# Turning an attention block's rows by transposing transfers of 16-bit planes, with scores two tiles ahead

## The chip, the cores and the metric

The kernel runs on one core of a Trainium2 chip. The metric is the device time of one launch in microseconds (us), lower is better. The core has a matrix engine (TensorE, here PE, with its weight loads as PEld), three elementwise engines (VectorE or DVE, ScalarE or ACT, GpSimd or POOL), and sixteen DMA engines that are fed through the queues of the issuing engines, here mostly SyncE (SP) and ScalarE. Each engine runs its instructions in order; they wait for each other through semaphores.

## The reference

The input x has 4 batches of 1024 rows of 1024 numbers. A recurrent stage makes new rows from x and a side input, by two scans along the 1024 positions (one forward, one backward), a division and a gate. Those rows then pass twice through the same attention over 16 slots per batch, and the result is added to x:

```python
for _ in range(NB):                      # NB = 2 blocks
    logits = _rms(x, norm_pre_w) @ compete_w.T + compete_b
    vals, idx = jax.lax.top_k(jnp.swapaxes(logits, 1, 2), 4)
    wgt = jax.nn.softmax(vals, axis=-1)
    wx = x @ write_w.T + write_b
    written = einsum('bsk,bskd->bsd', wgt, take_along_axis(wx, idx))
    ws = _rms(ws + written, norm_post_w)
    q  = x @ wq.T + bq                   # 16 heads of 64
    kk = ws @ wk.T + bk
    vv = ws @ wv.T + bv
    att = softmax(einsum('blhd,bshd->bhls', q, kk) * scale)
    ctx = einsum('bhls,bshd->blhd', att, vv)
    x = _rms(x + ctx @ out_proj_w.T + out_proj_b, norm_post_w)
```

All numbers are 32-bit floats. `_rms` divides a row by the root of its mean square and multiplies by a weight.

## The kernel before, in words

There are three stages: the recurrence (function bodies up to line 720), and then, for each of the two blocks, `write_slots` (the choice of rows, the slots, and the maps that attention needs) and `attention`. Before attention `write_slots` folds the query projection into the keys (`km`, 1024 by 256 for a batch, and 16 more columns in the first block for the next logits) and the output projection into the values (`vm`, 256 by 1024). So a tile of 128 rows needs two products only: its scores, rows times `km`, and its outputs, weights times `vm`. There are 32 tiles a block.

The order on every engine is the order in which the code is written (`pin`). The work on one tile g is:

- `load` (L1070): SP loads the rows `y`, and in the first block also the turned rows `xt`, 512 KB each. The turned rows are needed because PE contracts over the partitions. The recurrence makes them anyway and stores them in `turned_rows`. Three tiles are loaded in `begin_loads`; in the loop tile g + 3 is loaded in the pass of tile g.
- `turn_rows` (L1078), in the second block only: PE transposes the eight 128x128 squares of `y` (tile `ptr`), and ACT copies them from PSUM to `xt` in two copies.
- `scores` (L1090): PE, eight accumulated products into the bank `psc`.
- `softmax` and `softmax_sum` (L1104, L1121): DVE adds the bias, takes the maximum of each head and subtracts it; ACT takes the exponential; DVE sums and inverts; POOL multiplies.
- `turn_weights` (L1134): PE transposes the two squares of weights (`pet`), ACT copies them beside the weights.
- `output` (L1144): PE, two halves of two accumulated products into two banks `po`; DVE adds each half to `y`. The first block also computes the next logits (`poc`).
- `norm` (L1191): ACT sums the squares, DVE and POOL make the inverse root, DVE scales `y`. In the first block SP stores `y` to `rows[1]`, where the second block loads it from; in the second block POOL adds x (`xin`) and SP stores to the output.

In the pass of tile g, `run` (L1262) issues the loads for g + 3, the scores and softmax of g + 1, the outputs of g, the turned weights of g + 1 and the norm of g. In the second block the rows of g + 2 are turned between the scores of g + 1 and the outputs of g. Before the loop, `begin` does the scores and softmax of tile 0, and `early` turns the rows of tiles 0 and 1 of the second block while the rows chosen for the slots are being gathered.

SP runs its transfers in order as well: within one pass these are the loads, a weight load for the next block in some passes (`load_ahead`), and the store of the tile's rows after its norm. The row buffers are five, the buffers for turned rows three, those for scores and weights (`half`) two, those for 1 MB pieces of weights (`wide`) nine. `hold_clock` issues matmuls whose result nobody uses.

Of the kernel before, what the change touches and what calls it, by code (L numbers as in the profile page):

```python
# [11 lines left out]
U32 = mybir.dt.uint32  # L12
AF = mybir.ActivationFunctionType
# [5 lines left out]
P = 128  # L19
# [5 lines left out]
NT = L // P  # L25
# [13 lines left out]
def kernel(  # L39
# [37 lines left out]

    pin = tc.keep_in_program_order
# [7 lines left out]
    def wide(name):  # L86
        return weights.tile([P, 2, D], F32, tag="wide", bufs=9, name=name)
# [171 lines left out]
    with rec_stack:  # L259
# [276 lines left out]
        for i in range(N):  # L536
# [22 lines left out]
            if N // 2 - 2 <= i < N // 2 + 8 and i % 2 == 0:  # L559
                load_ahead(0, (i - N // 2 + 2) // 2)  # L560
            if i == N - 1:
                for n in range(5, 9):
                    load_ahead(0, n)
# [164 lines left out]
    def half_row(name):  # L728
        return work.tile([P, 2 * C + S], F32, tag="half", bufs=2, name=name)[:, : D // 2]
# [7 lines left out]
    def write_slots(blk, begin_loads, early, begin):  # L737
# [72 lines left out]
        hold_clock(bank("po", f"idle_rows{blk}"), 5 if first else 1)  # L810
# [33 lines left out]
        for n in range(5, NJ):  # L844
            wkv.append(load_kv(n, blk))
# [214 lines left out]
    def attention(blk):  # L1060
# [7 lines left out]
        lg_ps, maps = {}, {}  # L1068
# [9 lines left out]
        def turn_rows(g):  # L1078

            ptr = [turned(f"ptr{g}_{h}") for h in range(2)]  # L1080
            for h in range(2):
                for q in range(4):
                    pin(nc.tensor.transpose(ptr[h][:, q, :], y[g][:, ts(4 * h + q, P)], ident))  # L1083
            xt_g[g] = trow(f"xt{blk}_{g}").rearrange("p (k c) -> p k c", c=P)
            return [
                lambda h=h: pin(nc.scalar.copy(xt_g[g][:, 4 * h : 4 * h + 4, :], ptr[h]))
                for h in range(2)
            ]
# [15 lines left out]
        def softmax(g):  # L1104

            n = f"{blk}_{g}"
            two[g] = work.tile([P, 2 * C + S], F32, tag="half", bufs=2, name=f"e{n}")
            e = two[g][:, :C]
            w = C if last else C + S
            pin(nc.vector.tensor_add(two[g][:, :w], psc[g][:, :w], score_bias[:, g // NT, :w]))  # L1110
            e3 = e.rearrange("p (h s) -> p h s", s=S)
            mx = small.tile([P, H], F32, tag="mx", name=f"mx{n}")
            pin(nc.vector.tensor_reduce(mx, e3, AX.X, ALU.max))
            pin(
                nc.vector.tensor_tensor(
                    e3, e3, mx.unsqueeze(2).to_broadcast([P, H, S]), ALU.subtract
                )
            )
            pin(nc.scalar.activation(e, e, AF.Exp))
# [14 lines left out]
        def turn_weights(g):  # L1134
            if last:
                pet = bank(("aux", "lg")[g % 2], f"pet{blk}_{g}", 1)[:, :C]
            else:
                pet = turned(f"pet{blk}_{g}").rearrange("p q c -> p (q c)")[:, :C]
            pet = pet.rearrange("p (q c) -> p q c", c=P)
            for h in range(2):  # L1140
                pin(nc.tensor.transpose(pet[:, h, :], two[g][:, ts(h, P)], ident))  # L1141
            pin(nc.scalar.copy(two[g][:, C + S :].rearrange("p (h t) -> p h t", h=2), pet))  # L1142
# [106 lines left out]
        def early():  # L1249

            if last:
                for g in range(2):
                    for copy in turn_rows(g):
                        copy()

        def begin(km):
            maps["km"] = km
            scores(0)
            softmax(0)
            softmax_sum(0)  # L1260

        def run(vm, vmc):  # L1262
            maps["vm"], maps["vmc"] = vm, vmc
            turn_weights(0)
            for g in range(N + 1):
                here, next_, past = g < N, g + 1 < N, g > 0
                if g + 3 < N:
                    load(g + 3)
                if here and last:
                    xin[g] = fat(f"xin{g}")  # L1270
                    move(xin[g], x[g // NT, ts(g % NT, P), :])
                if not last and 4 <= g < 4 + 2 * 9 and g % 2 == 0:
                    load_ahead(blk + 1, (g - 4) // 2)
                if past and here and not last:
                    total_n = square_sum(y[g - 1], f"n{g - 1}")
                if next_:
                    scores(g + 1)
                    turn = last and g + 2 < N
                    if turn:
                        copies = turn_rows(g + 2)  # L1280
                        copies[0]()
                    softmax(g + 1)
                    if turn:
                        copies[1]()
                if past and next_ and not last:
                    inv_n = inverse_root(total_n, f"n{g - 1}")
                if next_:
                    softmax_sum(g + 1)
                if past and here and last:
                    pin(nc.gpsimd.tensor_add(y[g - 1], y[g - 1], xin[g - 1]))  # L1290
                    move(out[(g - 1) // NT, ts((g - 1) % NT, P), :], y[g - 1])
                if next_ and past and not last:
                    next_logits(g - 1, inv_n)
                if here:
                    output(g)
                if past and not last:
                    if here and not next_:
                        next_logits(g - 1, inverse_root(total_n, f"n{g - 1}"))
                    turn_logits(g - 1)
                    if here and not next_:  # L1300
                        hold_clock(bank("po", "idle_norm"), 4)
                if next_:
                    turn_weights(g + 1)
                if here:
                    (norm if next_ else norm_last)(g)
# [60 lines left out]
```

## Time and profile before

The time is 1098.41 us, the median of three runs (1097.13 to 1103.73).

| | |
|---|---|
| profiled execution's own time | 1097.41 us |
| its span, first to last instruction | 1095.6 us |
| instructions | 11962 |
| granted clock of PE, mean | 0.962 |
| DMA traffic | 218.79 MB, 200 GB/s over the span |
| first block's attention | about 508 to 756 us |
| second block's attention | about 816 to 1092 us |

A line of the profile's groups names the source line, the engine and the operation, the tiles (written <- read) with their shape, the number of such instructions, and the time of one. In an answer in order of time the first number is the start in us from the start of the span and the second the length; the square bracket gives the idle time of the engine before and what ended it. "SPq" is SP issuing a transfer: its length is the time to issue, and the landing is told apart. The chain of waits is the path that ended last, followed back from the end.

### The profile page before, as it was taken

Reading aid. Unit: us, or ns where it says so; the run is one execution under the profiler, and the core shown is the slowest. Engines: PE = TensorE matmul, PEld = TensorE weight load, DVE = VectorE, ACT = ScalarE, POOL = GpSimd, SP = SyncE. Lnnn points to the kernel's source line nnn. Section 1 sums busy time; section 2 is a strip of 40 time slices with the busy share of each in tenths; the row PEclk is TensorE's granted clock in tenths of the full one; section 3 lists DMA queues with packets and bytes.
Section 4 is the critical chain, followed back from the end, with each engine's and each line's share of the span. In section 5 each row is a group of like instructions: output and inputs, shape, how many; then the busy total and the mean of one; then the engine's idle time right before and its main releaser. Section 6 shows DMA issues by size and latency. Waiting matters only on the chain.

```text
span 1095.6 us, 11962 instructions
## 1 busy us (share of the span) xinstructions
PE 972.7 (89%) x4156; PEld 541.9 (49%) x4156; DVE 767.0 (70%) x1049; ACT 507.5 (46%) x787; POOL 546.4 (50%) x417
## 2 busy tenths in 40 slices
PE   2688788877878788899999999998999999999996
PEld 0123222222323233584666666664584676766763
DVE  7999999999999995144666666656144555555555
ACT  5476777768676763012334444444123333333332
POOL 4999999999999882100222222222100444434444
PEclk9789899989989899999999999999999999999999
DMA  8575574856564265790577777553760454545554
GB/s 272 181 261 170 155 225 128 281 153 232 171 212 129 82 200 156 256 355 16 203 277 281 267 253 273 205 200 120 282 260 20 149 216 179 213 188 208 192 210 154
DMA packets 121788, 218.79 MB, mean 200 GB/s; under 512 B 10928, under 2 KB 76592, under 8 KB 121728
## 3 DMA queue, kind: packets, MB, share of 16 engines
q1 hardware_dynamic: 87872, 199.15, 51.3%
q10 hardware_dynamic: 33280, 16.78, 5.3%
q0 software_dynamic: 576, 2.10, 0.5%
q8 instruction: 33, 0.54, 0.2%
q14 instruction: 27, 0.22, 0.1%
HBM read 150.90 MB, written 67.11 MB: 199 GB/s over the span
## 4 chain that ended last, share of the span: by engine, by line
PE 58%; DVE 31%; issue 4%; POOL 3%; ACT 2%; DMA 1%; SPq 0%; POOLq 0%; DVEq 0%; ACTq 0%
DVE both L320 22%; PE psc L1095 20%; PE po L1152 19%; DVE both L419 3%; DVE ov L364 3%; PE ptr L1083 3%; PE pk L955 3%; PE pkv L885 3%; PE pv L1023 2%; PE pet L1141 1%; PE pw L835 1%; PE raw L442 1%; PE poc L1168 1%; PE num L370 1%; PE pmix L817 1%
## 5 line engine op out<-in xcount | busy, mean ns | idle before, releaser
L1095 PE MATMUL psc<-km,xt 128*128 128x272 f32 (+1 forms) x1024 | 238.4, 386 | 0.0
L1152 PE MATMUL po<-vm,e 128*128 128x512 f32 x512 | 230.4, 593 | 0.9 <-ACT e L1142 0.9
L1095 PEld LDWEIGHTS psc<-km,xt 128*128 128x128 f32 x1024 | 189.5, 190 | 29.1
L370 PE MATMUL num<-ov,minus_ident 128*128 128x512 f32 x128 | 88.6, 831 | 97.6 <-DVE ov L364 97.6
L1129 POOL TENSOR_TENSOR e<-e,den 128x256 f32<-128x256 f32 x64 | 40.5, 633 | 252.5 <-DVE den L1127 231.4
L320 DVE TENSOR_TENSOR_SCAN both<-columns,edges,both 128x1024 f32<-128x1024 f32 x64 | 148.2, 2316 | 0.0
L1152 PEld LDWEIGHTS po<-vm,e 128*128 128x128 f32 x512 | 94.8, 190 | 95.7 <-issue 85.4
L1193 DVE SCALAR_TENSOR_TENSOR y<-y,inv,npost_bc 128x1024 f32<-128x1024 f32 x62 | 79.6, 1285 | 41.2 <-POOL inv L1188 41.2
L1161 DVE TENSOR_TENSOR y<-po,y 128x512 f32<-128x512 f32 x128 | 85.8, 674 | 30.9 <-PE po L1152 30.6
L1181 ACT ACTIVATE junk<-y 128x1024 f32<-128x1024 f32 x63 | 66.7, 1058 | 69.2 <-DVE y L1193 69.1
L370 PEld LDWEIGHTS num<-ov,minus_ident 128*128 128x128 f32 x128 | 28.2, 244 | 134.3 <-issue 67.7
L1188 POOL TENSOR_TENSOR inv<-mean,minus_half 128x1 f32<-128x1 f32 x64 | 35.5, 555 | 96.8 <-DVE mean L1186 96.8
L412 POOL TENSOR_TENSOR both<-both,quo 128x1024 f32<-128x1024 f32 (+1 forms) x33 | 75.7, 2295 | 14.9 <-ACT quo L399 14.0
L308 POOL TENSOR_TENSOR ekv<-ek,kf 128x1024 f32<-128x1024 f32 (+1 forms) x33 | 75.6, 2293 | 2.6
L1142 ACT COPY e<-pet 128x256 f32<-128x256 f32 x64 | 23.8, 371 | 113.1 <-PE pet L1141 112.9
L413 POOL TENSOR_TENSOR gate<-gate,quo 128x1024 f32<-128x1024 f32 (+1 forms) x33 | 75.3, 2283 | 0.0
L431 POOL TENSOR_TENSOR gate<-gate,both 128x1024 f32<-128x1024 f32 x31 | 73.3, 2366 | 1.2
L1290 POOL TENSOR_TENSOR y<-y,xin 128x1024 f32<-128x1024 f32 x31 | 73.1, 2358 | 1.4 <-DVE y L1193 1.4
L320 DVE TENSOR_TENSOR_SCAN both<-columns,ek 128x1024 f32<-128x1024 f32 (+1 forms) x32 | 71.5, 2234 | 2.0 <-POOL gate L431 2.0
L320 DVE TENSOR_TENSOR_SCAN both<-columns,ekv 128x1024 f32<-128x1024 f32 (+1 forms) x32 | 71.4, 2231 | 0.0
L442 PE MATMUL raw<-gate,lhs 128*32 128x512 f32 x128 | 69.3, 666 | 0.6 <-POOL gate L431 0.5
L1186 DVE TENSOR_SCALAR mean<-total 128x1 f32<-128x1 f32 x64 | 9.8, 153 | 85.1 <-ACT junk L1181 45.7
(203 smaller groups left out, 1536.9 us busy)
## 6 DMA issues: line engine op xcount, KB each, us to landing
y<-rows SPq DMA_DIRECT2D x64, 512.0 KB, 4.2
kf<-in_ft_dram SPq DMA_DIRECT2D x32, 512.0 KB, 5.3
gate<-in_xt_dram SPq DMA_DIRECT2D x32, 512.0 KB, 6.5
turned_rows<-gate SPq DMA_DIRECT2D x32, 512.0 KB, 3.5
xt<-turned_rows SPq DMA_DIRECT2D x32, 512.0 KB, 5.2
rows<-y SPq DMA_DIRECT2D x32, 512.0 KB, 2.9
xin<-in_x_dram SPq DMA_DIRECT2D x32, 512.0 KB, 4.5
rows<-stage ACTq DMA_DIRECT2D x31, 512.0 KB, 4.4
```

What stands on the lines that cost most here:

```text
L308: pin(nc.gpsimd.tensor_tensor(ekv[:, part], ek[:, part], kf[:, part], ALU.mult))
L320: nc.vector.tensor_tensor_scan(dst[:, way], dec, src[:, way], start, ALU.mult, ALU.add)
L370: nc.tensor.matmul(num_ps[:, ts(h, 512)], minus_ident, src[:, ts(h, 512)], start=first, stop=not first,)
L412: pin(nc.gpsimd.tensor_tensor(den, den, quo[:, part], ALU.mult))
L413: pin(nc.gpsimd.tensor_tensor(xk, xk, quo[:, part], ALU.mult))
L431: pin(engine.tensor_tensor(xk, xk, factor[:, part], ALU.mult))
L442: nc.tensor.matmul(raw[rows_b, ts(h, 512)], lhs[:, w].rearrange("p h s -> p (h s)"), src[:, ts(h, 512)], start=(k == 0 and w == k), stop=( ...
L1095: nc.tensor.matmul(psc[g][:, :n], xt_g[g][:, k, :], maps["km"][:, g // NT, k, :n], start=(k == 0), stop=(k == NK - 1),)
L1152: nc.tensor.matmul(po, et[:, ts(c, P)], vm[:, c, ts(h, 512)], start=(c == 0), stop=(c == 1),)
L1161: pin(nc.vector.tensor_add(half, po, half))
L1193: pin(nc.vector.scalar_tensor_tensor(y[g], y[g], inv[g], npost_bc, ALU.mult, ALU.mult))
L1290: pin(nc.gpsimd.tensor_add(y[g - 1], y[g - 1], xin[g - 1]))
```

## The change

The change replaces the way in which tiles 2 to 31 of the second block get their turned rows, and it moves the scores one more tile ahead in both blocks.

- In the first block, after its norm, ACT splits a tile `y` into two planes, the lower and the upper 16 bits of every number (`split`, one copy of 2048 16-bit elements on each partition), and SP stores the planes to a new tensor `planes` in DRAM, 512 KB a tile. The planes of tile g - 1 are split in the pass of g.
- In the second block ACT issues a transposing transfer of 16-bit elements, 128 rows by 2048 columns, from `planes` into a buffer of the weights' pool (`load_turned`), and later interleaves the two planes again into 32-bit numbers with one copy (`merge`). In the pass of g it merges g + 3 and issues the transfer for g + 5; the first three transfers and the first merge stand in `begin`. Tiles 0 and 1 are still turned on PE.
- The scores and softmax of g + 2 are done in the pass of g, in both blocks; `begin` does tiles 0 and 1. The turned weights of g are made at the start of its own pass, after the norm of g - 1, no longer at the end of the pass before. The tile loads stay at g + 3.
- There are three `half` buffers instead of two, and eight `wide` buffers instead of nine. So eight pieces of weights, not nine, are loaded ahead for each block, and the fifth piece of keys and values is loaded in `write_slots`.
- In `write_slots` the second block holds the clock with five matmuls instead of one.
- The split of tile 31 comes after the last logits, and the store of its planes ahead of the second block's loads on SP.

```diff
-        return weights.tile([P, 2, D], F32, tag="wide", bufs=9, name=name)
+        return weights.tile([P, 2, D], F32, tag="wide", bufs=8, name=name)
...
-        hold_clock(bank("po", f"idle_rows{blk}"), 5 if first else 1)
+        hold_clock(bank("po", f"idle_rows{blk}"), 5)
...
-        for n in range(5, NJ):
+        for n in range(4, NJ):
             wkv.append(load_kv(n, blk))
...
+        def load_turned(g):
+            pair[g] = weights.tile([P, 2, D], F32, tag="wide", bufs=8, name=f"pair{g}")
+            pair[g] = pair[g].bitcast(U16)[:, 0, :].rearrange("p (n c) -> p n c", c=P)
+            pin(
+                nc.scalar.dma_start_transpose(
+                    pair[g], planes[ts(g, P)].rearrange("r h d -> r (h d)")
+                )
+            )
+
+        def merge(g):
+            xt = trow(f"xt{blk}_{g}")
+            pin(
+                nc.scalar.copy(
+                    xt.bitcast(U16).rearrange("p (n h) -> p h n", h=2),
+                    pair[g].rearrange("p (h k) c -> p h (k c)", h=2),
+                )
+            )
+            xt_g[g] = xt.rearrange("p (k c) -> p k c", c=P)
+
+        def split(g):
+            two_planes = work.tile([P, 2, D], U16, tag="planes", name=f"planes{g}")
+            pin(
+                nc.scalar.copy(
+                    two_planes, y[g].bitcast(U16).rearrange("p (d h) -> p h d", h=2)
+                )
+            )
+            move(planes[ts(g, P)], two_planes)
...
         def begin(km):
             maps["km"] = km
-            scores(0)
-            softmax(0)
-            softmax_sum(0)
+            for g in range(2):
+                scores(g)
+                softmax(g)
+                softmax_sum(g)
+            if last:
+                for g in range(2, 5):
+                    load_turned(g)
+                merge(2)
```

The new loop as a whole:

```python
for g in range(N):
    ahead, end, past = g + 2 < N, g == N - 1, g > 0
    turn_weights(g)
    if g + 3 < N:
        load(g + 3)
    if last:
        xin[g] = fat(f"xin{g}")
        move(xin[g], x[g // NT, ts(g % NT, P), :])
    elif 4 <= g < 4 + 2 * 8 and g % 2 == 0:
        load_ahead(blk + 1, (g - 4) // 2)
    if past and not last:
        total_n = square_sum(y[g - 1], f"n{g - 1}")
    if ahead:
        scores(g + 2)
        softmax(g + 2)
    if past and not last:
        split(g - 1)
        inv_n = inverse_root(total_n, f"n{g - 1}")
    if last and g + 3 < N:
        merge(g + 3)
        if g + 5 < N:
            load_turned(g + 5)
    if ahead:
        softmax_sum(g + 2)
    if past and last:
        finish(g - 1)                      # POOL adds x, SP stores the output
    if past and not last:
        next_logits(g - 1, inv_n)
    output(g)
    if past and not last:
        turn_logits(g - 1)
    if end and not last:
        hold_clock(bank("po", "idle_norm"), 4)
    (norm_last if end else norm)(g)
if not last:
    turn_logits(N - 1)
    split(N - 1)
```

## The prediction

> **What bounds the kernel now.** I read the page's busy times first, then busy time by stretch, then the chain of waits and the timeline inside each attention stage. The page says that PE is the busiest engine; the stretches (560 to 740 us is the first block's attention, 840 to 1070 us the second's) say that there it has no idle time at all:
>
> ```profile
> PE 972.7 (89%) x4156; PEld 541.9 (49%) x4156; DVE 767.0 (70%) x1049; ACT 507.5 (46%) x787; POOL 546.4 (50%) x417
> ```
>
> ```profile
> 560.00:740.00 180.00, 180.00 (x716) 121.05 (x716) 112.25 (x277) 72.59 (x144) 39.52 (x69) 1.00 0.69 248
> 840.00:1070.00 230.00, 230.00 (x979) 159.83 (x978) 129.92 (x259) 86.89 (x174) 98.65 (x86) 1.00 0.49 186
> ```
>
> Columns of the second fence: length, busy PE, PEld, DVE, ACT, POOL, granted clock, DMA share, GB/s. One tile of the second block, by the chain:
>
> ```profile
> 883.73 0.22 PE pet L1141 x2
> 883.95 3.46 PE psc L1095 x16
> 887.40 0.87 PE ptr L1083 x8
> 888.27 3.44 PE po L1152 x8
> ```
>
> That is the whole period: 0.22 + 3.46 + 0.87 + 3.44 = 7.99 us. A first-block tile has 3.67 of scores, 3.44 of outputs and 0.69 of small matmuls (poc, lg, pet): 7.79. The first block also has a path through SP, which the page doesn't show. Timeline of one tile, and the landing time of the turned rows:
>
> ```profile
> 602.43 0.51 PE L1168 MATMUL poc<-vmc,e 128*128 128x16 f32 x4
> ...
> 603.59 1.06 ACT L1181 ACTIVATE junk<-y 128x1024 f32<-128x1024 f32 x1
> ...
> 605.59 1.28 DVE L1193 SCALAR_TENSOR_TENSOR y<-y,inv,npost_bc 128x1024 f32<-128x1024 f32 x1 [0.66 <-POOL inv L1188]
> ...
> 606.90 0.32 SPq L81 DMA_DIRECT2D rows<-y  x1
> ...
> 607.31 0.38 SPq L81 DMA_DIRECT2D y<-rows  x1
> ...
> 607.79 0.73 SPq L81 DMA_DIRECT2D xt<-turned_rows  x1
> ...
> 610.91 3.83 PE L1095 MATMUL psc<-km,xt 128*128 128x272 f32 x16
> ```
>
> ```profile
> DMA to landing us min/median/max: 4.9/5.2/5.5
> ```
>
> See here: SP issues the next loads only when the store of the tile just normalised has gone out, at 606.90, when the norm ends. The turned rows issued at 607.79 land at 613.0. The scores that start at 610.91 are of a tile loaded one period earlier; those that need 613.0 start at 618.7, so 5.7 us are spare.
>
> **What the change does to the first block.** Scores go two tiles ahead, the loads stay three ahead. The rows loaded in tile g's pass are now needed in the next pass, not the one after: the start moves from 618.7 to 610.9 while the landing stays at 613.0. So PE waits for a DMA. The loop, from the end P of the outputs of tile g: the turned weights' copy no longer lies ahead of the sum of squares (saves 0.2 of the 4.44 from 602.43 to the norm's end at 606.87): norm ends P + 4.25; xt issue 0.92 later (606.87 to 607.79), P + 5.17; landing 5.2, P + 10.4; 0.1 to the matmul; 3.67 + 3.44 to the end of the outputs two tiles on: P + 17.6. Two tiles in 17.6 us is 8.8 each, against 7.79: 1.0 us for each of the 28 tiles 4 to 31 (tile 3 is issued with no store ahead), 28 us. The landing's 4.9 to 5.5 gives 24 to 33.
>
> The split joins ACT: 32 copies of 2048 elements. ACT's rows 128x512 at 630 ns and 128x4096 at 3618 have a slope of 0.834 ns, so 1.91 us each (no 16-bit row is in the trace; 1.9 if strided halves run like words, perhaps double if not, never less than the 1.06 of a 1024 row). It stands behind the exponential, where ACT (72.6 of 180 us) is free, and ends at about P + 9.3, 0.5 ahead of the next sum of squares: nothing, except that every fourth tile the logits' row (0.68) now follows it and pushes the squares, about 2 us in all. At double it would be on the path with 1.4 us a tile. The planes' store (512 KB, 1.48 us of 16 engines from the SP queue's 51.3% for 199 MB, 0.32 of SP) goes out before the norm ends and is down when the loads start; DMA goes from 0.69 x 7.79 = 5.4 to 6.9 us of 8.8. First block: +30.
>
> **The second block.** Out: 30 groups of eight transposes, 30 x 0.87 = 26 us of PE, and 60 copies of 0.58 us. If PE stayed the bound, the tile would take 7.12. But the merge (1.91 by the same slope) is put behind the exponential, and the next scores wait for it:
>
> ```profile
> 932.44 1.06 ACT L1181 ACTIVATE logits<-y 128x1024 f32<-128x1024 f32 x1 [0.18 <-DVE y L1161]
> ...
> 934.44 1.28 DVE L1193 SCALAR_TENSOR_TENSOR y<-y,inv,npost_bc 128x1024 f32<-128x1024 f32 x1 [0.66 <-POOL inv L1188]
> ...
> 935.64 0.42 DVE L1110 TENSOR_TENSOR e<-psc,score_bias 128x256 f32<-128x256 f32 x1
> ...
> 937.06 0.42 ACT L1119 ACTIVATE e<-e 128x256 f32<-128x256 f32 x1 [0.70 <-DVE e L1115]
> ```
>
> From the first DVE add to the end of the exponential are 1.84 us, to the end of the merge 3.66. The add starts 0.2 after the scores end (S); PE is done with outputs and pet at S + 3.66; the merge is seen at S + 4.0. So 0.35 us of PE wait remain: period 7.47. A second loop stands beside it: merge, issue of the next transposing transfer on ACT, sum of squares, norm (3.28 from 932.44 to 935.72), add to merge's end (3.66 less 0.07 overlap): 6.9 us plus the issue. So the issue's time D decides from 0.55 on. The trace has ACT's plain transfer at 366 ns. The Trainium skill (DMA: Bandwidth & Descriptors, the sequencer table within "Why a DMA increments its semaphore by 16 and not by 1") puts a small transposing instruction of the older generations at 631 cycles where a copy takes 512: scaled by the row, 0.45. The same table's case with one push per tile is 32 cycles a tile, and 128 tiles of 16 x 128 would make 2.9. Lower end 0.37, upper 2.9; I take 0.7, nearer to the row because it is one instruction. Period 7.6, against 7.99: 30 x 0.38 = 11 us less. At 2.9 it is 9.8: 55 us more.
>
> The transfer itself: the ACT queue's 512-byte packets cost 5.3% of 1095.6 us for 32 transfers, 1.81 us each; a line through that queue (28 ns a packet) and SP's (102 ns for 2.27 KB) gives 2.3 us at 256 bytes. With 0.49 x 7.99 = 3.9 of other traffic that is 6.2 of 7.6 us: hidden, and two passes (15 us) lie between issue and merge. A rule speaks against it: VectorE: DVE Perf Modes, "The three transpose paths", has 1309 ns for one 128x128 square by DMA against 390 on TensorE. Here PE's eight 32-bit squares take 0.87; the DMA must do sixteen, which at 1309 one after another is 21 us a tile, +400 us. Another page (Advanced Engine Details and Errata, "X-Bar Transpose (TRN2)") calls such transfers as fast as plain ones. I hold 1309 for mostly the fixed part of one small transfer, as 512 KB land here in 2.9 to 5.2 us, and take 2.3.
>
> **Costs paid once.** (a) Between the blocks, SP holds the second block's loads behind the store of the last planes, whose split ends 1.9 us after the last logits: loads start at 765.4 instead of 762.1, the early transposes 3 us later; and holding PE's clock takes five matmuls of 0.9 (the four of idle_norm take 3.60) instead of one, ahead of pmix at 771.36: 770.2 + 3.1 + 4.5 = 777.8. About 6 us. (b) At the second block's start, ACT issues three transposing transfers and waits in the first merge for about 5 us of landing; queued behind it are the vm copies, and PE has two banks: about 6 us. (c) Without scores between them, the last outputs follow each other at the norm's pace: 0.5 us in each block. (d) One weight buffer less loads ahead: one more 1 MB load per block lands inside the mixing and projections, whose loads have several us in hand: 0, or 2.9 us a block if the cover is gone.
>
> Sum: 1097.4 (the profiled execution; span 1095.6) + 30 - 11 + 6 + 6 + 1 = 1129; the median shown lies 1 above, so 1130.
>
> **The rivals.** *Issue or transfer too slow:* as above, but D between 1 and 2.9 or a transfer over 3.5 us of 16 engines (then 3.9 + 3.5 fills the period). 1130 + 30 x (D - 0.7): 1139 to 1196, beyond if the 1309 holds. For it: the upper price and a queue shared with loads. Against: 0.366. *The planes are cheap and the rows come in time:* the landing would have to be so short that the first block keeps 7.79; with 7.12 in the second 1097 - 26 + 13 = 1084, faster; the point is a landing of 3.1 us against the 4.9 seen at least (the store of rows ahead of it takes 2.9). With 7.5 in the second instead, 1096, no change. Against: it is the second 512 KB of a pair in one queue. *PE fully bound:* the stages keep PE at 100%, so only PE time counts and 26 us go: 1071. Against: the two new waits above.
>
> **How the numbers follow.** Late rows with D up to 1: 0.55, 1120 to 1140. Issue or transfer slow: 0.32. No loss or little: 0.08 within 1%. Faster, the last two rivals together: 0.05. The range leaves out both ends: 1110 to 1195. 1% is about what a measurement here tells from no change.
>
> **What would show it.** In the first block, scores 8.8 us apart and waiting for the DMA of xt by 1 us a tile; if 7.8, my main step is wrong. In the second, scores 7.6 apart, no ptr after the first 16, the scores' wait on ACT's merge; the merge's row at 1.9; ACT's transposing issue between 0.37 and 2.9. pmix starts 6 us later after the norm than now. I am wrong above all if the transposing transfers take several us of the engines or delay the plain loads in their queues.

## The result: slower by 6.6%

The changed kernel takes 1175.42 us (median of four runs, 1163.33 to 1181.46) beside 1097.77 for the kernel before on the same chip: a ratio of 1.066, 95% interval 1.056 to 1.076. The ratio leaves out the slowest run, 1181.46 us, because it lies more than 1.5% above the fastest. The direction is the one forecast and the time lies within the range, but the 78 us added are more than twice the 32 forecast. The profiled execution took 1177.8 us, its span 1176.0, so 80.4 us of span have to be found.

The page's busy times of the changed kernel. PE is as busy as before in microseconds, and idle for 75 us more:

```profile
PE 978.1 (83%) x3924; PEld 530.1 (45%) x3924; DVE 767.8 (65%) x1049; ACT 599.4 (51%) x789; POOL 546.5 (46%) x417
```

Busy time by stretch, of the two attention loops and of two tiles of the first (length, busy PE, PEld, DVE, ACT, POOL, granted clock, DMA share, GB/s):

```profile
521.00:785.00 264.00, 236.33 (x887) 157.33 (x887) 138.31 (x340) 139.27 (x206) 48.83 (x85) 0.96 0.69 255
910.00:1150.00 240.00, 212.54 (x746) 137.31 (x745) 130.12 (x258) 120.07 (x144) 98.27 (x86) 0.99 0.79 237
531.09:540.66 9.57, 9.57 (x31) 6.45 (x32) 4.45 (x10) 3.35 (x4) 1.36 (x3) 0.82 0.49 180
540.66:548.55 7.89, 7.89 (x33) 5.18 (x31) 5.00 (x13) 4.76 (x7) 1.72 (x3) 1.00 0.59 212
```

PE waits in both loops, where it had no idle time before. The third and fourth lines are two tiles within which PE does not wait at all. The first starts at the end of a wait of 1.89 us and takes 9.57 us, the other takes 7.89. What sets them apart is the granted clock, 0.82 beside 1.00.

One pair of tiles of the first block in order of time:

```profile
600.43 0.75 SPq L85 DMA_DIRECT2D xt<-turned_rows  x1
...
603.18 0.38 PE L1170 MATMUL pet<-ident,e 128*128 128x128 f32 x2
...
605.84 3.93 PE L1127 MATMUL psc<-km,xt 128*128 128x272 f32 x16 [2.28 <-DMA xt<-turned_rows]
607.06 0.32 SPq L85 DMA_DIRECT2D rows<-y  x1
...
607.95 0.74 SPq L85 DMA_DIRECT2D xt<-turned_rows  x1
...
613.73 3.83 PE L1127 MATMUL psc<-km,xt 128*128 128x272 f32 x16
```

The load issued at 600.43 is needed at 603.6 and lands over 5 us after its issue. The scores of the next tile follow at once, 7.89 us on, and the ones after that wait again, 9.70 us on. That is the loop of the forecast, two tiles long, and here, where the clock holds, it takes the 17.6 us forecast for it.

One tile of the second block, where the merge and the issue of the transfer meet on ACT:

```profile
978.51 4.25 ACTq L1097 DMA_TRANSPOSE pair<-planes  x1
...
978.79 2.49 ACT L1105 COPY xt<-pair 128x2048 uint16<-128x2048 uint16 x1
...
981.33 3.72 PE L1127 MATMUL psc<-km,xt 128*128 128x256 f32 x16 [1.46 <-ACT xt L1105]
...
982.88 1.06 ACT L1210 ACTIVATE logits<-y 128x1024 f32<-128x1024 f32 x1 [1.60 <-issue]
```

PE waits for the merge. The sum of squares behind it waits for the issue, which begins beside the merge, 0.3 us before it, and outlasts it by 1.5 us. All the transfers and merges (duration in ns, least, median, most):

```profile
L1097 ACTq DMA_TRANSPOSE pair<-planes x30: 1332/2324/4856, 880.1 to 1128.3; - x30
L1105 ACT COPY xt<-pair x30: 2462/2477/2488, 888.5 to 1144.7; 128x2048 uint16<-128x2048 uint16 x30
```

The added span by stage, from the starts of the scores on PE. The new order moves one tile's scores from each loop to the stage ahead of it, and leaves one tile's outputs to the stage behind it. They are no added time, so they are taken off where they now stand (4.13, 3.46 and 3.66 us). A loop is 29 tiles. The rows add up to 81 us. One tile's transposes, 0.9 us, fall away besides, and that leaves the 80.4 but for rounding.

| stage | before | after | added | forecast |
|---|---|---|---|---|
| first loop, a tile | 7.80 | 9.24 | 29 x 1.44 = 41.8 | 30 |
| last scores of the first block to first of the second | 72.2 | 89.6 | 17.4 - 4.1 = 13.2 | 6.5 |
| first scores of the second block to its loop | 19.9 | 33.0 | 13.1 - 3.5 = 9.6 | 6 |
| second loop, a tile | 7.98 | 8.38 | 29 x 0.40 = 11.5 | -11 |
| last scores to the end | 20.2 | 28.8 | 8.6 - 3.7 = 4.9 | 0.5 |

### The profile page after: what moved, and what is told of

The parts are those of the page before. It is cut to its first block, busy times and chain, and to the rows that moved or that the text cites. A ratio compares the mean times of both kernels' runs of the same rounds, so it can differ in the third digit from the quotient of the medians.

```text
span 1176.0 us, 11657 instructions
## 1 busy us (share of the span) xinstructions
PE 978.1 (83%) x3924; PEld 530.1 (45%) x3924; DVE 767.8 (65%) x1049; ACT 599.4 (51%) x789; POOL 546.5 (46%) x417
## 5 line engine op out<-in xcount | busy, mean ns | idle before, releaser
L1127 PE MATMUL psc<-km,xt 128*128 128x272 f32 (+1 forms) x1024 | 254.7, 404 | 55.1 <-DMA xt<-turned_rows 27.6
L1127 PEld LDWEIGHTS psc<-km,xt 128*128 128x128 f32 x1024 | 197.4, 198 | 99.1 <-ACT xt L1105 34.4
L1181 PE MATMUL po<-vm,e 128*128 128x512 f32 x512 | 234.1, 600 | 7.3 <-ACT e L1171 7.3
L1181 PEld LDWEIGHTS po<-vm,e 128*128 128x128 f32 x512 | 98.0, 192 | 106.5 <-issue 79.6
L1151 ACT ACTIVATE e<-e 128x256 f32<-128x256 f32 x64 | 26.6, 416 | 186.7 <-DVE e L1147 133.9
L1217 POOL TENSOR_TENSOR invn<-mean_n,minus_half 128x1 f32<-128x1 f32 x32 | 17.6, 551 | 136.0 <-DVE mean_n L1215 136.0
L1105 ACT COPY xt<-pair 128x2048 uint16<-128x2048 uint16 x30 | 74.3, 2476 | 8.4 <-issue 8.4
L1142 DVE TENSOR_TENSOR e<-psc,score_bias 128x272 f32<-128x272 f32 (+1 forms) x64 | 27.6, 431 | 74.4 <-PE psc L1127 74.4
```

What stands on the lines that cost most here:

```text
L1105: nc.scalar.copy(xt.bitcast(U16).rearrange("p (n h) -> p h n", h=2), pair[g].rearrange("p (h k) c -> p h (k c)", h=2),)
L1127: nc.tensor.matmul(psc[g][:, :n], xt_g[g][:, k, :], maps["km"][:, g // NT, k, :n], start=(k == 0), stop=(k == NK - 1),)
L1181: nc.tensor.matmul(po, et[:, ts(c, P)], vm[:, c, ts(h, 512)], start=(c == 0), stop=(c == 1),)
```

## The experiments

Each is an edit of the changed kernel. Runs with a ratio were timed in turns with the kernel before. The others ran once, and are read by their stages, since two executions of the changed kernel can differ by over 14 us. The granted clock is given for the stretch named.

**The turned rows, loaded one pass earlier.** `xt` gets a load of its own, four tiles ahead of the pass instead of three.

```diff
-            if not last:
-                xt_g[g] = trow(f"xt{g}").rearrange("p (k c) -> p k c", c=P)
-                move(xt_g[g], turned_rows[g // NT][g % NT])
+        def load_xt(g):
+            xt_g[g] = trow(f"xt{g}").rearrange("p (k c) -> p k c", c=P)
+            move(xt_g[g], turned_rows[g // NT][g % NT])
...
                     load(g + 3)
+                if not last:
+                    for n in (3, 4) if g == 0 else (g + 4,):
+                        if n < N:
+                            load_xt(n)
```

> The changed kernel with the turned rows of the first block loaded four tiles ahead instead of three (same three buffers; the rows y stay three ahead). Theory 1, late rows: PE no longer waits for the transfer of xt, the first block's scores stand 7.8 us apart as before the change, its granted clock is 1.00, and the time falls by 38 to 42 us to about 1135. Theory 2, the split on ScalarE and the store of the planes fill the first block: scores stay 9 us or more apart and the time falls by less than 10.

Measured: 1141.04 us, ratio 1.040 (1.037 to 1.043), 34 us less. PE waits for no turned row any more, the clock of the first loop is 1.00, and 22 of its 29 tiles take 7.7 to 7.9 us. The other seven, in the middle of the block where weights are loaded too, take 8.6 to 9.4. One of them in order of time:

```profile
608.28 1.90 ACT L1117 COPY planes<-y 128x2048 uint16<-128x2048 uint16 x1 [2.71 <-DMA planes<-planes]
...
611.13 0.35 ACT L1172 COPY e<-pet 128x256 f32<-128x256 f32 x1
...
611.54 3.70 PE L1182 MATMUL po<-vm,e 128*128 128x512 f32 x8 [0.35 <-ACT e L1172]
```

The split waits 2.71 us for the store of the planes before, because there is one buffer for planes; the squares and the copy that the outputs need stand behind it on ACT. So theory 1 holds for the late rows, which were the main cost of the first block. Behind them a second wait was hidden, 8 us in all.

**An idle matmul in the gap.** One matmul whose result nobody uses stands ahead of each tile's scores in the first block.

```diff
                 if ahead:
+                    if not last:
+                        hold_clock(bank("po", f"fill{g}"), 1)
                     scores(g + 2)
```

> The changed kernel with one matmul of 512 columns whose result nobody uses (0.86 us) ahead of the scores in each pass of the first block. Theory A, PE's clock falls because of the waits: the waits are shorter, the clock is granted in full, and scores stand 8.9 to 9.0 us apart on average instead of 9.3, 8 to 12 us less in all, although PE has 28 us more work. Theory B, the clock falls for another cause: scores 9.3 or more apart, the time the same or up to 24 us longer.

Measured: 1162.42, and theory A. The first loop takes 8.98 us a tile instead of 9.24, 7.7 us less although PE has more to do, and its clock is 1.00 instead of 0.96. No tile takes 9.57 any more. So part of the first block's loss was not waiting but slow work after the wait. The second block is unchanged in this kernel. In this execution its tiles took 8.06 or 8.07 us but for the first (7.88) and one of 8.12, 9 us less in all: the irregular tiles there come and go.

**No split, the same stores.** ACT's split is left out; the store carries a tile of zeros.

```diff
-            two_planes = work.tile([P, 2, D], U16, tag="planes", name=f"planes{g}")
-            pin(
-                nc.scalar.copy(
-                    two_planes, y[g].bitcast(U16).rearrange("p (d h) -> p h d", h=2)
-                )
-            )
-            move(planes[ts(g, P)], two_planes)
+            if g == 0:
+                pair["zero"] = work.tile([P, 2, D], U16, tag="planes", name="zero_planes")
+                pin(nc.gpsimd.memset(pair["zero"].rearrange("p h d -> p (h d)").bitcast(F32), 0.0))
+            move(planes[ts(g, P)], pair["zero"])
```

> The changed kernel without ScalarE's split: a tile of zeros is stored as every tile's planes, so the second block's rows are wrong for tiles 2 to 31, while all transfers and all other instructions stay. Theory 1, late rows: the first block stays within 5 us, scores about 9.3 us apart with the same waits for xt; only the end of the first block, where the last split holds up SyncE's queue, becomes some 3 to 7 us shorter. Theory 2, the split is on the first block's path: scores 8.3 us apart or less and 25 us or more off the time.

Measured: 1200.17, slower than either theory had it. The order of time says why:

```profile
629.62 0.74 SPq L85 DMA_DIRECT2D xt<-turned_rows  x1
630.41 0.46 SPq L85 DMA_DIRECT2D planes<-zero_planes  x1
...
635.72 4.48 PE L1124 MATMUL psc<-km,xt 128*128 128x272 f32 x11 [2.70 <-DMA xt<-turned_rows]
```

Without the split to wait for, the planes' store goes out right behind the load of the turned rows and shares the DMA engines with it. The rows now land after 6.0 us (median) instead of 5.2, and the first loop's clock falls to 0.92. So the split itself is not on the loop's path. It had kept the store out of the load's way, 2.7 us behind its issue instead of 0.8. Between the blocks the stretch falls from 89.6 to 84.8 us, within what theory 1 allowed there: the last split had held up SP's loads.

**Rows turned by TensorE again.** No planes at all; the new order of the pass stays.

```diff
...
-                    split(g - 1)
...
-                if last and g + 3 < N:
-                    merge(g + 3)
-                    if g + 5 < N:
-                        load_turned(g + 5)
...
                 output(g)
+                if last and g + 3 < N:
+                    turn_rows(g + 3)
```

> Block 1's rows are turned by TensorE again (eight transposes and two copies to a tile, behind the outputs), and no planes are split, stored or loaded; the scores and the softmax stay two tiles ahead. Theory A, block 0's rows are late because the planes' stores share the DMA with them: the waits of TensorE for turned rows in block 0 fall below 5 us, its tile to 7.8 us, and the time to 1100 to 1110. Theory B, they are late because the new order of the pass issues each load one pass before its use, planes or not: waits of 20 us or more stay, the tile stays at 8.8 us or above, and the time is 1130 to 1145.

Measured: 1176.81, ratio 1.066 (1.059 to 1.074): as slow as the whole change, and 32 us above even theory B's time. PE's waits in the first loop (us in total, times, longest):

```profile
PE psc L1127 <- DMA xt<-turned_rows: 26.7, 14, 2.3
```

The DMA share of that loop is 0.56 instead of 0.69, and the waits are 26.7 us all the same, the tile 9.15. So theory B has the cause right: the rows are late because of the order, not because of the planes' traffic. What it missed is the second block, where the tile takes 8.5 to 9.3 us, against 7.98 before with the same transposes: in this order, scores two ahead bring nothing where TensorE turns the rows.

**The transfer without transposing.** The planes are loaded by a plain transfer of the same size, so the second block's rows are not turned.

```diff
-                nc.scalar.dma_start_transpose(
-                    pair[g], planes[ts(g, P)].rearrange("r h d -> r (h d)")
+                nc.scalar.dma_start(
+                    pair[g], planes[ts(g, P)].rearrange("r h (n c) -> r (h n) c", c=P)
```

> The changed kernel with plain transfers of the planes in place of the transposing ones, same bytes, same ScalarE queue; the rows are then not turned, so tiles 2 to 31 of the second block are computed from wrong rows. Theory C, the transposing instruction itself is slow to issue: ScalarE issues in 0.4 to 0.5 us, no tile of the second block is over 8.2 us apart, all stand at 8.07 (the merge's loop), and with 6 us off the start of that block the time falls by 14 to 18 us. Theory D, ScalarE's issue waits because the DMA engines are loaded: issues of over 1 us remain and less than 8 us is gained.

Measured: 1161.78, and the issue on ACT:

```profile
L1097 ACTq DMA_DIRECT2D pair<-planes x30: 326/327/388, 879.8 to 1112.2; - x30
```

0.33 us instead of 1.3 to 4.9. The tiles of the second loop take 8.06 to 8.08 us after the first one, and the stretch ahead of the loop is 6.6 us shorter. So theory C holds: the issue of a transposing transfer is what is slow here, and the merge, still 2.48 us, sets the 8.07.

**The merge the other way round.** It reads scattered and writes in line.

```diff
-                    xt.bitcast(U16).rearrange("p (n h) -> p h n", h=2),
-                    pair[g].rearrange("p (h k) c -> p h (k c)", h=2),
+                    xt.bitcast(U16).rearrange("p (n h) -> p n h", h=2),
+                    pair[g].rearrange("p (h k) c -> p (k c) h", h=2),
```

> The merge writes its 16-bit elements in line and reads them scattered, the other way round than in the changed kernel; the rest is unchanged. Theory A, the scattered 16-bit writes make the merge 2.48 us where the split, which reads scattered and writes in line, is 1.88: the merge falls to about 1.9 us, the undisturbed tile of block 1 from 8.06 to about 7.5 us, the time by about 15 us to 1160. Theory B, an access of two elements at a time costs as much as a scattered write: the merge stays at 2.4 us or more, the tile at 8.06 and the time at 1175.

Measured: 1168.1. The merge takes 2.118 us (2.111 to 2.124), the undisturbed tile 7.70 to 7.71. Between the two theories: of the 0.57 us by which the merge exceeds its forecast, 0.36 go when the writes are in line and the reads scattered, and 0.2 stay. The undisturbed tile follows the merge exactly, 8.06 - 0.36.

**SyncE issues the transfers.**

```diff
-                nc.scalar.dma_start_transpose(
+                nc.sync.dma_start_transpose(
```

> The transposing transfers are issued by SyncE instead of ScalarE. Theory A, their issue of 1.3 to 4.9 us on ScalarE holds back square, sum and copy behind it: all tiles of block 1 at about 8.06 us, the stretch from the first scores of block 1 to those of its third tile 6 to 8 us shorter, the time about 16 us lower, near 1160. Theory B, the issue only moves its harm, since SyncE's loads of x and y and its stores now stand behind it: tiles of block 1 stay irregular, with waits for DMA in place of issue, and the time stays above 1170.

Measured: 1169.78. The beginning of the second block takes 23.38 us, which is before's 19.92 and the moved 3.46: its whole excess is gone. The loop runs at 8.06 for fourteen tiles, but 8.1 to 10.3 in the second half, with PE waiting for the merge. On this queue the issue is longer still:

```profile
L1097 SPq DMA_TRANSPOSE pair<-planes x30: 1582/4279/5552, 860.4 to 1126.7; - x30
```

Theory A holds for the beginning, theory B for the later tiles.

**The merge ahead of the scores.** With SyncE's issue, `merge` and `load_turned` move ahead of `scores(g + 2)` in the pass.

```diff
+                if last and g + 3 < N:
+                    merge(g + 3)
+                    if g + 5 < N:
+                        load_turned(g + 5)
                 if ahead:
                     scores(g + 2)
                     softmax(g + 2)
...
-                if last and g + 3 < N:
-                    merge(g + 3)
-                    if g + 5 < N:
-                        load_turned(g + 5)
```

> As the run with SyncE's issue, and the merge of tile g+3 stands ahead of the scores and the exp of tile g+2 instead of behind them. Theory A, the tile of 8.06 us is the chain exp, merge, square, copy of the turned weights on ScalarE, which the merge lengthens only where it stands behind the exp: the tile falls to what TensorE has to do, 7.1 to 7.4 us, and the time by 20 to 28 us more than with SyncE's issue alone, to about 1135. Theory B, the merge is only moved, and delays the exp by as much: the tile stays near 8.0 us and the time near 1160.

Measured: 1171.56, neither. Six tiles take 7.11 us, TensorE's own time, the next three 7.3 to 7.6, and then, once the transfers issued in advance are used up, 8.2 to 10 us. The merge's group says for what:

```profile
L1105 ACT COPY xt<-pair 128x2048 uint16<-128x2048 uint16 x30 | 74.8, 2495 | 31.7 <-DMA pair<-planes 31.7
```

It now waits for the transposed planes. The DMA share of the loop is 0.79 to 0.83, so the engines are not full. What is full is SP. In its order stand the store of a finished tile, the load of a row whose buffer that same store must leave first (it lands after 3.1 us), 1.1 us for two issues, and 4.3 for the transposing one: about 8.6 us a tile. The loop still gains 7 us over the run before it, but after the last scores the kernel takes 36.1 us instead of 27.6, and that takes them back.

**One idle matmul between the blocks**, as before the change.

```diff
-        hold_clock(bank("po", f"idle_rows{blk}"), 5)
+        hold_clock(bank("po", f"idle_rows{blk}"), 5 if first else 1)
```

> One idle matmul of TensorE between the blocks instead of five, the rest as changed. Theory A, they stand on the path behind the transposes of block 1's first rows: 89.6 us from the last scores of block 0 to the first of block 1 become about 85, the time 5 us less. Theory B, the slots' product waits for something else by then, or runs at a lower granted clock without them: 88 us or more, the time unchanged.

Measured: 1184.73, with 92.9 us between the blocks, where the change has 89.6: theory B. PE with one idle matmul (two records), and then the changed kernel's with five (ten):

```profile
823.49 1.97 PE L1087 MATMUL ptr<-ident,y 128*128 128x128 f32 x8 [4.31 <-DMA y<-rows]
...
827.82 1.92 PE L119 MATMUL idle_rows<-npost_bc,ident 128*128 128x512 f32 x2
829.53 6.93 PE L821 MATMUL pmix<-spare,spare 128*128 128x64 f32 x32
836.92 9.74 PE L839 MATMUL pw<-ww,mix_t 128*64 128x512 f32 x32 [0.46 <-ACT mix_t L829]
```

```profile
818.15 1.97 PE L1087 MATMUL ptr<-ident,y 128*128 128x128 f32 x8 [4.47 <-DMA y<-rows]
...
822.05 4.75 PE L119 MATMUL idle_rows<-npost_bc,ident 128*128 128x512 f32 x10
826.64 3.68 PE L821 MATMUL pmix<-spare,spare 128*128 128x64 f32 x32
830.79 7.09 PE L839 MATMUL pw<-ww,mix_t 128*64 128x512 f32 x32 [0.46 <-ACT mix_t L829]
```

The four idle matmuls fewer save 2.8 us, and the slots' two products (`pmix`, `pw`) take 5.9 us more: the granted clock over them is 0.63, and 1.00 with five. Both follow a wait of over 4 us for `y`. So the five earn their time as long as that wait stands; the cost is the wait.

**Everything mended, in two forms.** Turned rows four ahead; two buffers for planes (paid for with one row buffer; the rows `y` of both blocks then load two ahead); one idle matmul; the merge ahead of the scores and written in line; every third row of the second block in the planes' buffers, so that no load waits for the store just issued. In one form SyncE issues all transposing transfers; in the other ScalarE does in the loop, and SyncE the first three, which land before ScalarE's first is issued.

```diff
-        return work.tile([parts, D], F32, tag="row", bufs=5, name=name)
+        return work.tile([parts, D], F32, tag="row", bufs=4, name=name)
...
-            y[g] = row(f"y{blk}_{g}")
+            if last and g % 3 == 2:
+                y[g] = work.tile([P, 2, D], U16, tag="planes", bufs=2, name=f"y{blk}_{g}")
+                y[g] = y[g].rearrange("p h d -> p (h d)").bitcast(F32)
+            else:
+                y[g] = row(f"y{blk}_{g}")
...
```

> The change with its harms taken away one by one: turned rows of block 0 loaded four tiles ahead and rows two ahead, two buffers for the planes, one idle matmul between the blocks as before the change, the merge ahead of the scores with its writes in line, the transfers issued by SyncE, and rows of block 1 in two rings, so that the load of a row no longer waits for the store of the tile before last. Theory A, the irregular tiles of 8.6 us in the second half of block 1 are SyncE's own chain (store out, 3.1 us until it has landed and frees a row, loads 1.1, issue 4.3): tiles of block 0 at 7.79 us, 42 us less; between the blocks 5 less; start of block 1 10 less; tiles of block 1 at 7.1 to 7.3, some 33 less: 1175 - 90 = 1085 us. Theory B, the DMA engines can't bring 2 MB a tile with a quarter of it transposed any faster, whatever issues it: tiles of block 1 stay at 8.3 to 8.8 us and the time is 1115 to 1130.

> As the run with everything mended, but ScalarE issues the transposing transfers within block 1's loop, behind the merge (only the first three are SyncE's). Theory A, what ScalarE has to do in a tile fits under TensorE's 7.1 us as long as the issue takes 2.3 us (exp 0.42, merge 2.12, square 1.24, copy 0.35, issue 2.3: 6.4): tiles at 7.1 us with single ones at 8 to 9 where the issue takes more than 3: 1085 to 1095 us. Theory B, the issue grows to 3 to 5 us as the tiles get shorter, since it is paced by the DMA engines: ScalarE becomes the bound, tiles at 8 us or more, 1110 to 1125 us.

Measured: 1093.41 (ratio 0.997, 0.995 to 0.999) and 1094.39 (0.996, 0.995 to 0.998). Every tile of the first loop takes 7.7 to 7.8 us. In the second, six take 7.11 and the rest 7.3 to 7.5, nearly all 7.45, in both forms. The same 60 us of the loop by stretch, first with SyncE's issue, then with ScalarE's:

```profile
940.00:1000.00 60.00, 59.36 (x210) 37.38 (x209) 35.81 (x74) 30.85 (x40) 27.57 (x24) 1.00 1.04 282
```

```profile
940.00:1000.00 60.00, 59.35 (x210) 37.38 (x209) 35.85 (x73) 31.20 (x41) 27.58 (x24) 1.00 0.91 282
```

Neither theory's end. The irregular tiles were the queues, but the tile stops at 7.45 us, 0.34 above TensorE's own time, whichever engine issues. The DMA share is 1.04 in one form and 0.91 in the other, which makes the DMA engines an unlikely cause, and the chain of waits settles it. Of the form with SyncE's issue:

```profile
945.34 0.52 POOL inv L1222
...
945.88 1.28 DVE y L1227
947.16 0.35 DVE e L1147
...
948.52 0.43 ACT e L1156
...
949.86 0.61 POOL e L1166
950.47 2.31 POOL y L1348
952.78 0.52 POOL inv L1222
```

From one inverse root on POOL to the next are 7.44 us: the norm, the softmax of the next scores, the softmax's multiplication on POOL, and then, ahead of the next inverse root, the addition of x to the finished rows (L1348, 2.31 us). Neither a transfer nor TensorE stands in this loop. Its POOL steps have this spacing from the first tile on, and TensorE takes 7.11 only while its lead lasts. This is read from the trace; no run moved the addition to another place.

The loop has gained 17 us over before, yet the kernel only 4: between the blocks it still loses 10.2 us (86.5 for 72.2, less 4.1) and at the end 8.4. In the profiled executions the span is 2.9 us shorter, and 2.6 of these lie ahead of the first scores, a stretch that differs by up to 8 us between the runs here.

**The two ends.** For the last two tiles the turned weights come ahead of the norm; the last split and its store come behind the loads of the second block's first rows, which get buffers that are free by then.

```diff
-                turn_weights(g)
+                if g < N - 2:
+                    turn_weights(g)
...
+                if N - 3 <= g < N - 1:
+                    turn_weights(g + 1)
                 (norm_last if end else norm)(g)
...
-                split(N - 1)
+                late.append(lambda: split(N - 1))
...
             begin_loads()
+            late.pop()()
+        junk = row(f"junk{blk}", R)
+        kv = row(f"kv{blk}")
```

> As the run with everything mended and SyncE's issue, and the two ends of each block put right: for the last two tiles, which have no scores to cover it, the copy of the turned weights stands ahead of the norm's square on ScalarE; the split and the store of the last planes stand behind the loads of block 1's first two rows, which take buffers that are free by then. Theory A, the ends hold the 10 us between the blocks and the 8 us at the end that the mended kernel still has over before: waits of TensorE for the copy 1.6 and 2.2 us between the blocks, as much at the end, with low clock behind them, and 4.9 us for the rows: 12 to 16 us less, 1078 to 1082 us. Theory B, behind each of these waits stands another that is as late (norm, store and top-k of the last tile are one chain): 5 us less or nothing, 1088 to 1093 us.

Measured: 1086.62, ratio 0.991 (0.988 to 0.994): 0.9% faster than the kernel before, 6.8 us less than without this edit by the medians and 9.4 by the profiled spans. Between the two theories. PE at the end of the first block:

```profile
744.83 3.70 PE L1187 MATMUL po<-vm,e 128*128 128x512 f32 x8 [0.46 <-ACT e L1177]
748.37 0.51 PE L1203 MATMUL poc<-vmc,e 128*128 128x16 f32 x4
750.41 0.28 PE L1272 MATMUL lg<-ident,lgs 128*16 128x128 f32 x1 [1.53 <-DVE lgs L1261]
...
769.01 3.39 PE L1093 MATMUL ptr<-ident,y 128*128 128x128 f32 x16 [1.48 <-DMA y<-rows]
```

The wait for the copy falls from 1.6 to 0.46 us, and 1.53 of waiting for the next logits take its place; the wait for the rows falls from 4.1 to 1.5 and, with a second wait of 0.8 that goes, gives 3.4. The last norm, the top-k and the gather are one chain by the code; no run tried to shorten it.

## Why the prediction was right in direction and short in size

**Late rows in the first block: right, 28 us forecast and 27.6 measured.** The page has it in the group of the scores:

```profile
L1127 PE MATMUL psc<-km,xt 128*128 128x272 f32 (+1 forms) x1024 | 254.7, 404 | 55.1 <-DMA xt<-turned_rows 27.6
```

The two-tile loop of 17.6 us, the landing of 5.2 us, and the cause in the order of the loads all held. What failed is the step from "P + 10.4; 0.1 to the matmul" to the end of the outputs, which priced the work after a wait at full speed. The whole loop was forecast 30 us longer and is 41.8. In six tiles that follow a wait the clock is 0.82, 1.69 us each, 10 of the 12 us missing here; the idle matmul showed it by giving 7.7 back.

**The split costs nothing: right.** Its row is 1.88 us (1.91 forecast), and leaving it out did not help. What the forecast did not see is that it spaces the DMA traffic, and that its one buffer would come onto the path once the rows are in time.

**The second block: the right two terms, both too small; 22.5 of the 48 us missing in the profiled executions.** This is the step that failed most. The merge was priced by "the same slope" as the split, 1.91 us. It takes 2.48, and the period forecast as 7.47 becomes 7.47 + 0.57 = 8.04; measured 8.06. Against the 7.6 taken, that is 29 x 0.46 = 13 us. The other 9 us are the issue. D was taken as 0.7 between bounds of 0.37 and 2.9, "nearer to the row because it is one instruction". It was 2.32 in the median, near the other end, and up to 4.86. The nearest row in kind was a plain transfer, and that was the wrong neighbour. The loop's form was off too: "merge, issue of the next transposing transfer on ACT, sum of squares" adds the two, but the trace shows them beside each other, from 978.51 and 978.79. The sum is then 6.9 less 1.91 plus the longer of the two: at 4.25 us, 9.24, and the tile measured there is 9.04. By this sum the issue decides only from about 3.1 us. With the added form a median of 2.3 would have made 9.2 of every tile, so the rival "Issue or transfer too slow", whose 1130 + 30 x 1.62 = 1179 us lies near the result by luck, had the right engine but not the right place. Its second half, a transfer that fills the DMA engines, did not come true: the transfer was priced at 2.3 us of the sixteen engines and took 2.66, and in the form with everything mended no transfer stands in the chain of waits.

**Between the blocks: 6.5 forecast, 13.2 measured.** (a) named the loads held behind the last planes' store, and that is so: 4.47 us of waiting for `y`, where the kernel before has no wait, and 4.8 us less when the planes are zeros and no split holds their store. Before, and the changed kernel:

```profile
766.86 3.30 PE L1083 MATMUL ptr<-ident,y 128*128 128x128 f32 x16
```

```profile
818.15 1.97 PE L1087 MATMUL ptr<-ident,y 128*128 128x128 f32 x8 [4.47 <-DMA y<-rows]
```

It also booked the five idle matmuls as a cost; after such a wait they are worth more than they take. The tails, (c), were put at "0.5 us in each block" and cost about 5 each. The outputs do follow at the norm's pace, but the copy of the turned weights stands behind the squares on ACT, which makes PE wait 1.6 to 2.1 us twice, and one group of outputs then runs at 5.4 instead of 3.7 us (granted clock 0.68). The end of the kernel before, and of the changed one:

```profile
1083.67 3.70 PE L1152 MATMUL po<-vm,e 128*128 128x512 f32 x8 [0.46 <-ACT e L1142]
```

```profile
1156.62 5.40 PE L1181 MATMUL po<-vm,e 128*128 128x512 f32 x8 [2.05 <-ACT e L1171]
```

**The start of the second block: 6 forecast, 9.6 measured.** The vm copies behind the first merge were right. The wait was not the landing but three issues in a row on ACT; from SyncE the whole excess is gone.

```profile
880.06 8.39 ACTq L1097 DMA_TRANSPOSE pair<-planes  x3
888.49 2.46 ACT L1105 COPY xt<-pair 128x2048 uint16<-128x2048 uint16 x1 [8.37 <-issue]
```

**PE fully bound (1071): it exists for six tiles** of 7.11 us. Behind it stands the loop through POOL, 7.45 us a tile, which neither this rival nor the forecast had: in this order the transposes could give 0.5 us a tile, not 0.87.

## What to carry to other kernels

Moving work one tile ahead moves the deadline of everything that it reads: move the loads with it, or the old lead becomes a wait, and price the work behind that wait at a lower clock. For an operation that no trace shows, the nearest row can be the wrong neighbour: the plain transfer's 0.33 us said nothing of the transposing one's 2.32. Time it by itself first, beside its plain form, and ask where on its queue it stands. And before booking what a bound gives when it goes, add up the loops through the other engines, for the longest of them is what remains.

## What was not expected of the hardware

- **The clock falls after short waits.** Behind six of fourteen waits of 1.7 to 2.4 us in the first loop, a tile ran at a granted clock of 0.82: 9.57 x 0.18 = 1.7 us lost. The length of the wait does not decide, since one of 1.66 us is among the six and one of 2.28 is not. The Trainium skill (TensorE: Matmul & The Clock Gate, "What's actually happening") has the clock halved after an idle window of about 3.4 us, so these waits should be free. By an estimate from that page's figure, one window at half speed loses 1.7 us. The size of the loss agrees with the page; how short a wait brings it does not.
- **A transposing transfer takes long to issue**: 1.3 to 4.9 us on ScalarE and 1.6 to 5.6 on SyncE (up to 7.1 with everything mended), beside 0.33 for a plain one of the same size. What stands behind it on the queue waits; the copy handed over just before it ran beside it. Why it varies so was not tried. The load of the DMA engines alone is not it: on ScalarE with everything mended it took at most 2.55 us, though they moved more there (282 GB/s between 940 and 1000 us, where the changed kernel has 237 in its second loop).
- **It also costs the DMA engines more.** From the queue of its own in the second loop: 31.3% of 190 us for 11.73 MB, which is 2.66 us of all sixteen engines for a transfer of 0.524 MB; the plain ones, 17.7% for 12.45 MB, 1.42. The statement of the Trainium skill that such transfers are as fast as regular ones (Advanced Engine Details and Errata, "X-Bar Transpose (TRN2)") is not borne out for this shape.
- **The time of a copy of 2048 16-bit elements on ScalarE depends on which side is scattered.** The split, with scattered reads, takes 1.88 us; the merge takes 2.12 with scattered reads and 2.48 with scattered writes.
